# A graph layer's edge loop: groups taken in pairs, and one product that takes the transfer waits

## Chip, core and metric

One core of a Trainium2 chip runs the kernel. The core has a matrix engine (TensorE, called PE), a vector engine (DVE), a scalar engine (ACT), a general engine that also issues the indirect transfers (POOL), and a sync engine that issues the plain transfers (SP). Each has its own stream of instructions; they wait for one another by semaphores. Sixteen DMA engines move data between the chip's memory (DRAM) and the on-chip memory (SBUF); PE writes to PSUM, which has eight banks. The metric is the device time of one execution in microseconds (us).

## What is computed

A message-passing layer over a graph with 12500 nodes of 64 numbers and 200000 edges. `dst` is sorted.

```python
nodes = node_state[edges].reshape(num_edges, -1)          # x[src] | x[dst], 128 wide
gates = ssp(edge_state @ We1 + be1) @ We2 + be2
gates = gates * (1.0 - sigmoid(5.0 * (distance - 3.5)))
h = ssp(nodes @ Wn1 + bn1) @ Wn2 + bn2
messages = h * gates
message_sum = zeros_like(node_state).at[edges[:, 1]].add(messages)
new_state = node_state + (ssp(message_sum @ Ws1 + bs1) @ Ws2 + bs2)
out = layernorm(x + new_state)
```

`ssp(v)` is softplus less log 2. All arrays are fp32.

## The kernel before

**Groups.** The edges go through in 391 groups of 512 (`GE`), each in two halves of 256 (`HE`) and four columns of 128 (`K`). Because `dst` is sorted, the edges of one half touch a window of at most 42 neighbouring nodes (`W`). So `x[dst]` needs no gather: the lower half of Wn1 is multiplied with all nodes once, ahead of the loop (L508), and put in a table in DRAM; a half loads the 42 rows of its window, and a one-hot matrix picks the rows by a matrix product. The same one-hot matrix adds the messages up by node.

**One group, step by step.**

- `gather` (L186): four indirect transfers issued by POOL fetch `x[src]` of 128 edges each into `xg`. In twelve groups (`by_rows`) only three are indirect; the last 128 rows come one by one from SP (`fetch`, L201), four in each step of the loop.
- `load` (L207, L214): SP fetches the edge block `eT` and the two window rows `wns`.
- `onehot` (L219): DVE writes the one-hot columns beside the gathered ones.
- `transposes` (L227): PE transposes the four columns into the PSUM tile `tx`; `xcopy` (L232): ACT copies it to `xT`.
- `layer1_edge` (L236, L238) and `layer1_node` (L244): PE makes the first layers of gate and node net, 256 and 512 columns, into the PSUM tile `z` (two banks).
- `exps`, `logs` (L255, L258): ACT makes log(1 + exp(z)) over 768 columns; `softplus` (L263): DVE takes care of large values and writes `s`.
- `layer2_edge` (L269, L272), `layer2_node` (L278): PE makes the second layers into the PSUM tile `gh`.
- `hcut` (L287), `message` (L291): DVE multiplies by the cutoff and by each other.
- `scatter` (L295): PE multiplies messages and one-hot columns, into a free part of a `z` tile; `window` (L311): DVE adds the result to the running sums at the window's place, which it reads into a register with `window_bases` (L302).

That makes 28 products on PE for a group.

**Order.** The order is written out by hand. Step i of the loop handles several groups at different stages: second layer of group i-1, first layer of i+1, transposes of i+3, scatter of i-3, one-hot of i+5, load of i+5 and gather of i+16 (`AHEAD`). Each engine gets its instructions in the order in which the step writes them. The gather of group i+16 takes the buffer of group i-4 (20 buffers, `AHEAD + BEHIND`), so POOL waits there for the scatter of that group. The PSUM tiles z, gh and tx have two buffers each, eight banks in all. When all edges of a block of 512 nodes are done, the node net of that block is worked into the following steps in parts (`node_block`; L330 and L361 are its products). The last ten groups go in another order (`CATCH_UP`).

**Start.** Ahead of the loop stand the preparations: constants, the bases of the windows, the table, and the gathers of the first 16 groups.

Of the kernel before, what the change touches and what calls it, by code (L numbers as in the profile page):

```python
# [40 lines left out]
F32 = mybir.dt.float32  # L43
BF16 = mybir.dt.bfloat16
I32 = mybir.dt.int32
AF = mybir.ActivationFunctionType
OP = mybir.AluOpType
AX = mybir.AxisListType
PSUM = bass.MemoryType.PSUM
DRAM = bass.MemoryType.DRAM  # L50
DVE = mybir.EngineType.DVE
SP = mybir.EngineType.SP
# [4 lines left out]
P = 128  # L57
D = 64
HE = 256
GE = 2 * HE  # L60
W = 42
DW = D + W
PIECES = 3
NB = 512
K = 4
AHEAD = 16
LOADS = 5
SPREADS = 5
CATCH_UP = 10
PREPARE = 5  # L70
FREE = 7
BEHIND = 4

# [33 lines left out]
def gnn_resnorm_kernel(ctx: ExitStack, tc: tile.TileContext, a: dict, out: bass.AP, E: int):  # L107
# [16 lines left out]
    psum = ctx.enter_context(tc.tile_pool(name="psum", bufs=2, space=PSUM))  # L124

    def z_tile():
        return psum.tile([P, 2, NB], F32, name="z")

# [3 lines left out]
    def tx_tile():  # L132
        return psum.tile([P, NB], F32, name="tx")
# [31 lines left out]
    rs3 = const.tile([PIECES, K, D], BF16, name="rs3")  # L165
    wns = const.tile([DW, REST, 2, 2 * D], F32, name="wns")

# [5 lines left out]
    def padding(g, k):  # L173
        return g * GE + k % 2 * HE + k // 2 * P >= E

    def gather(g, after=False):

        xg = loads.tile([P, K, P], F32, name="xg", bufs=AHEAD + BEHIND)
        xgs[g] = xg
        if after:  # L180
            nc.vector.memset(xg[:, 0, :1], 0.0)
        for k in range(K - (g in by_rows)):
            if padding(g, k):
                nc.vector.memset(xg[:, k, :D], 0.0)
                continue
            nc.gpsimd.indirect_dma_start(  # L186
                out=xg[:, k, :D], out_offset=None, in_=x,
                in_offset=bass.IndirectOffsetOnAxis(ap=src_i[:, g, k : k + 1], axis=0))
# [13 lines left out]

    bases = {}

    def load(g):
        eTs[g] = loads.tile([P, HE], F32, name="eT")
        nc.sync.dma_start(eTs[g], a["eT"][:, g, :])  # L207
        if g % 2 == 0:
            _, at = nc.values_load_multi_w_load_instructions(
                base_i[0:1, 2 * g : 2 * g + 4], engines=[SP], min_val=0, max_val=N - 1,  # L210
                skip_runtime_bounds_check_because="they were clamped to these bounds")
            bases[g], bases[g + 1] = at[:2], at[2:]
        for h in range(2):
            nc.sync.dma_start(wns[D:DW, g % REST, h, :], table[bass.ds(bases[g][h], W), :])  # L214

    xTs, zs, us, ss, ghs, hs, msgs, scs = ({} for _ in range(8))

    def onehot(g):
# [3 lines left out]

    def transposes(g):
        tx = tx_tile()[:DW].rearrange("f (k e) -> f k e", k=K)
        for k in range(K):
            row = xrs[g][:, :DW] if g in by_rows and k == K - 1 else xgs[g][:, k, :DW]
            nc.tensor.transpose(tx[:, k, :], row, ident)  # L227
        xTs[g] = tx

    def xcopy(g):  # L230
        xT = work.tile([DW, K, P], F32, name="xT", bufs=3)
        nc.scalar.copy(xT, xTs[g])  # L232
        xTs[g] = xT.rearrange("f (t h) e -> f h t e", h=2)

    def layer1_edge(g):
        nc.tensor.matmul(zs[g][:, 0, :HE], be3.rearrange("q h d -> q (h d)"), ones3, start=True, stop=False,  # L236
                         skip_group_check=True)
        nc.tensor.matmul(zs[g][:, 0, :HE], we1.rearrange("a h d -> a (h d)"), eTs[g], start=False, stop=True,  # L238
                         skip_group_check=True)

    def layer1_node(g):
        for h in range(2):
            zn = zs[g][:, h, HE * (1 - h) : HE * (2 - h)]
            nc.tensor.matmul(zn, wns[:, g % REST, h, :], xTs[g][:, h], start=True, stop=True,  # L244
                             skip_group_check=True)
# [6 lines left out]
    def exps(g, part=every):  # L252
        if part.start == 0:
            us[g] = work.tile([P, 3 * HE], F32, name="u")
        nc.scalar.activation(us[g][:, part], z_of(g)[:, part], AF.Exp)  # L255
# [4 lines left out]
    def softplus(g, part=every):  # L260
        if part.start == 0:
            ss[g] = work.tile([P, 3, 2, P], F32, name="s", bufs=3)
        nc.vector.scalar_tensor_tensor(ss[g].rearrange("p i t e -> p (i t e)")[:, part], us[g][:, part], BIG,  # L263
                                       z_of(g)[:, part], OP.min, OP.max)

    def layer2_edge(g):
        gh = gh_tile()
        v = gh.rearrange("p (i t h d) -> p i t h d", i=2, t=2, h=2)
        nc.tensor.matmul(gh, ones3[:, :P], row3.rearrange("q i k d -> q (i k d)"), start=True, stop=False,  # L269
                         skip_group_check=True)  # L270
        for t in range(2):
            nc.tensor.matmul(v[:, 0, t], ss[g][:, 0, t, :], we2, start=False, stop=False, skip_group_check=True)  # L272
        ghs[g] = gh.rearrange("p (i k d) -> p i k d", i=2, k=K)

    def layer2_node(g):
        for h in range(2):
            for t in range(2):
                nc.tensor.matmul(ghs[g][:, 1, 2 * t + h, :], ss[g][:, 1 + h, t, :], wn2, start=False,  # L278
                                 stop=h == 1 and t == 1, skip_group_check=True)
# [5 lines left out]
    def hcut(g):  # L285
        hs[g] = work.tile([P, K, D], F32, name="h")
        nc.vector.tensor_mul(hs[g], ghs[g][:, 1], cut[:, g, :].to_broadcast([P, K, D]))  # L287

    def message(g):
        msgs[g] = work.tile([P, K, D], F32, name="msg", bufs=3)  # L290
        nc.vector.tensor_mul(msgs[g], ghs[g][:, 0], hs[g])  # L291

    def scatter(g, sc):
        for t in range(2):
            nc.tensor.matmul(sc, msgs[g][:, 2 * t : 2 * t + 2, :].rearrange("p h f -> p (h f)"),  # L295
                             xgs[g][:, 2 * t : 2 * t + 2, D:DW], start=t == 0, stop=t == 1, skip_group_check=True)
        scs[g] = sc

    window_at = {}

    def window_bases(g):
# [99 lines left out]
    with tc.manual_schedule():  # L401
# [3 lines left out]
        nc.sync.dma_start(src_i[:, AHEAD:, :], cols[:, AHEAD:, :])  # L405
        with tc.tile_pool(name="prep", bufs=1) as prep:
            dst_h = prep.tile([P, NR, HE], I32, name="dst_h")
# [19 lines left out]
            for g in range(AHEAD):  # L427
                if g < FREE:
                    gather(g)
                else:  # L430
# [10 lines left out]
            nc.scalar.dma_start(consts[:, FIRST:], a["consts"][:, FIRST:])  # L441
            nc.scalar.dma_start(wns[:D].rearrange("f r h o -> f (r h) o"),
                                a["Wn1"][:D, :].rearrange("f (r o) -> f r o", r=1).to_broadcast([D, 2 * REST, 2 * D]))

# [84 lines left out]

        with tc.tile_pool(name="finish", bufs=1) as finish:  # L530
            blocks = list(zip(node_blocks(N), block_steps(N, NG)))
# [9 lines left out]
            for i in range(-3, NG):  # L541
                second[i] = lagging(i, 1, (ends + 3,))
                third[i] = lagging(i, 3, (ends - 2, ends + 5))
                ahead[i] = [i + 3] if i < ends else [i + 2] if i == ends + 1 else [i + 1] if i > ends + 2 else []
            parts, begun, complete, rest = {}, None, 0, []

            def at(f, g, *more):
                if 0 <= g < NG:
                    f(g, *more)

            for g in range(LOADS - 3):
                load(g)
            for g in range(2):
                onehot(g)
            for i in range(-3, last - 1):
                now = parts.pop(i, [])
                early = [part for part in now if part.tensor]
                at(load, i + LOADS)
                fetch(i)
                if i >= 0:  # L560
                    at(gather, i + AHEAD, i < BEHIND)
                if i < ends:
# [49 lines left out]
                for part in now:  # L612
                    if not part.tensor:
                        part.others()
                complete = third[i][-1] + 1 if third[i] else 0
                if blocks and complete >= blocks[0][1] - PREPARE and not begun:
                    begun = node_block(*blocks[0][0], finish)
                    begun.pop(0).others()
                if blocks and complete >= blocks[0][1]:
                    steps = next(steps for steps in BLOCK_STEPS if i + steps[-1] < last - 1)  # L620
                    for n, part in zip(steps, begun):
                        parts.setdefault(i + n, []).append(part)
                    rest = begun[len(steps) :]
                    blocks.pop(0)
                    begun = None
            assert len(blocks) == 1 and begun and not parts
# [37 lines left out]
            for part in begun:  # L664
# [4 lines left out]
                         skip_runtime_bounds_check_because="a comparison's result")  # L669
    with tc.If(far > 0), tc.tile_pool(name="outside", bufs=1) as o:  # L670
        iota_n = o.tile([P, NB], F32, name="iota_n")
# [141 lines left out]
```

## Time and profile before

| what | before |
|---|---|
| median of three runs | 2455.14 us (2455.06 to 2465.51) |
| the profiled execution | 2482.05 us, its span 2480.3 us |
| mean granted clock of PE | 0.861 |
| PE busy | 2138.7 us, 86% of the span |
| POOL busy | 1473.3 us, 59%, 1555 instructions |
| DVE, ACT busy | 1087.5 us (44%), 920.1 us (37%) |
| DMA | 143.07 MB, mean 58 GB/s |
| first exp of the edge loop | 99 us after the start |
| last gather on POOL's timeline | starts at 2382 us |

The span runs from the first to the last instruction of the profiled execution; the time around it includes what lies before and after. "Busy" counts an engine while an instruction runs on it; a PE product's end is modelled, so a busy PE need not be at its full rate. The granted clock is the share of PE's full clock that the chip allowed. In the group rows, the number after the second bar is the idle time of the engine just ahead of these instructions, with what ended it: `<-PE z L244` means that the wait ended by a signal of PE about that product, `issue` means that the engine waited for nothing that the profile shows.

### The profile page before, as it was taken

How to read it: one execution, taken by the hardware profiler on the slowest of the kernel's cores; microseconds unless marked ns; L12 is line 12 of the kernel's file. 1: busy time of each engine (PE TensorE's matmuls, PEld its weight loads, DVE VectorE, ACT ScalarE, POOL GpSimd, SP SyncE). 2: the span in 40 equal slices, each digit the busy share in tenths (PEclk: the TensorE clock that was granted, in tenths of full speed). 3: DMA queues.
4: the chain of work that ended last, by engine and by line, in shares of the span. 5: the costliest groups of instructions: out<-in, count | busy, mean ns of one | idle time of the engine just before them, and what ended most of it. 6: DMA issues, size and time to landing. Idle time of an engine off the chain costs nothing.

```text
span 2480.3 us, 41084 instructions
## 1 busy us (share of the span) xinstructions
PE 2138.7 (86%) x11373; PEld 1741.1 (70%) x11373; DVE 1087.5 (44%) x2744; ACT 920.1 (37%) x1317; POOL 1473.3 (59%) x1555
## 2 busy tenths in 40 slices
PE   3888898889888989888988988888889888888897
PEld 3767677777767777767767776677767676676775
DVE  3334434444344344444444444444444444444455
ACT  1223333333333333433433333433333333433443
POOL 6656666666666666666666666666665656666620
PEclk9988879887888878898897888988887989988898
DMA  6322222222222222222222222222222222222220
GB/s 187 111 50 53 51 51 52 53 52 51 53 51 55 53 51 53 55 53 53 55 54 56 52 53 55 55 56 55 53 57 55 50 55 56 57 60 55 55 53 22
DMA packets 170982, 143.07 MB, mean 58 GB/s; under 512 B 46475, under 2 KB 142915, under 8 KB 170746
## 3 DMA queue, kind: packets, MB, share of 16 engines
q1 hardware_dynamic: 119746, 87.95, 12.3%
q0 software_dynamic: 49632, 50.92, 11.5%
q10 hardware_dynamic: 1368, 1.51, 0.3%
q8 instruction: 93, 1.52, 0.3%
q14 instruction: 143, 1.17, 0.2%
HBM read 130.57 MB, written 9.63 MB: 57 GB/s over the span
## 4 chain that ended last, share of the span: by engine, by line
PE 79%; issue 9%; DVE 5%; ACT 3%; another core or an unknown queue 3%; DVEq 1%; DMA 1%; SPq 0%; ACTq 0%
PE z L244 17%; PE gh L278 12%; PE gh L272 11%; PE z L238 11%; PE tx L227 8%; PE z L295 8%; PE gh L269 4%; PE z L236 3%; PE tx L330 2%; DVE h L287 1%; DVE msg L291 1%; ACT u L255 1%; DVE sums L311 1%; PE z L508 1%
## 5 line engine op out<-in xcount | busy, mean ns | idle before, releaser
L186 POOL DMA_INDIRECT xg<-in_x,src_i x1551 | 1473.1, 950 | 909.8 <-issue 360.3
L255 ACT ACTIVATE u<-z 128x768 f32<-128x768 f32 x392 | 317.4, 810 | 1435.4 <-PE z L244 466.8
L287 DVE TENSOR_TENSOR h<-gh,cut 128x256 f32<-128x256 f32 x391 | 166.0, 425 | 1154.0 <-PE z L244 357.8
L244 PE MATMUL z<-xT,wns 106*128 106x256 f32 x1564 | 498.4, 448 | 3.8 <-issue 1.6
L278 PE MATMUL gh<-consts,s 128*128 128x64 f32 x3128 | 429.6, 285 | 7.4 <-issue 7.4
L278 PEld LDWEIGHTS gh<-consts,s 128*128 128x128 f32 x3128 | 424.1, 210 | 6.9 <-issue 6.8
L272 PE MATMUL gh<-consts,s 128*128 128x128 f32 x1564 | 308.9, 325 | 133.8 <-issue 124.4
L244 PEld LDWEIGHTS z<-xT,wns 106*128 106x128 f32 x1564 | 353.0, 227 | 72.7 <-issue 4.2
L272 PEld LDWEIGHTS gh<-consts,s 128*128 128x128 f32 x1564 | 227.6, 210 | 240.4 <-issue 224.8
L263 DVE SCALAR_TENSOR_TENSOR s<-u,z 128x768 f32<-128x768 f32 x392 | 372.7, 951 | 24.3 <-ACT u L258 12.3
L258 ACT ACTIVATE u<-u,one 128x768 f32<-128x768 f32 x392 | 365.9, 934 | 12.7
L227 PE MATMUL tx<-consts,xg 128*106 128x128 f32 x1552 | 279.9, 308 | 61.0 <-ACT u L258 25.6
L238 PE MATMUL z<-eT,consts 128*128 128x256 f32 x782 | 313.9, 487 | 0.0
L295 PEld LDWEIGHTS z<-xg,msg 128*128 128x128 f32 x1512 | 279.8, 230 | 41.1 <-issue 8.2
L295 PE MATMUL z<-xg,msg 128*128 128x84 f32 x1512 | 263.4, 301 | 14.5 <-issue 14.2
L227 PEld LDWEIGHTS tx<-consts,xg 128*106 128x106 f32 x1552 | 211.3, 160 | 86.8 <-issue 46.0
L232 ACT COPY xT<-tx 106x512 f32<-106x512 f32 x391 | 221.6, 567 | 18.4 <-PE tx L227 11.2
L311 DVE TENSOR_TENSOR sums<-sums,z 64x42 f32 x756 | 148.7, 197 | 129.9 <-issue 118.4
L291 DVE TENSOR_TENSOR msg<-gh,h 128x256 f32<-128x256 f32 x391 | 165.8, 424 | 13.4
L238 PEld LDWEIGHTS z<-eT,consts 128*128 128x128 f32 x782 | 131.4, 211 | 54.1 <-issue 15.4
L269 PE MATMUL gh<-row,ones 3*128 3x512 bf16 x391 | 157.1, 402 | 2.7 <-DVE msg L291 2.6
L219 DVE TENSOR_TENSOR xg<-consts,rel 128x168 f32<-128x168 f32 x391 | 137.0, 351 | 0.1
(100 smaller groups left out, 621.4 us busy)
## 6 DMA issues: line engine op xcount, KB each, us to landing
eT<-in_eT SPq DMA_DIRECT2D x391, 128.0 KB
xg<-in_x,src_i POOLq DMA_INDIRECT x1551
xr<-in_x SPq DMA_DIRECT2D x1536, 0.2 KB
wns<-table SPq DMA_DIRECT2D x782, 21.0 KB
table<-tb SPq DMA_DIRECT2D x14, 448.0 KB
sums<-in_xT SPq DMA_DIRECT2D x7, 455.0 KB
y<-in_x SPq DMA_DIRECT2D x24, 128.0 KB
out<-y SPq DMA_DIRECT2D x24, 128.0 KB
```

The source lines that it names most:

```text
L186: nc.gpsimd.indirect_dma_start(out=xg[:, k, :D], out_offset=None, in_=x, in_offset=bass.IndirectOffsetOnAxis(ap=src_i[:, g, k : k + 1], ax ...
L227: nc.tensor.transpose(tx[:, k, :], row, ident)
L232: nc.scalar.copy(xT, xTs[g])
L238: nc.tensor.matmul(zs[g][:, 0, :HE], we1.rearrange("a h d -> a (h d)"), eTs[g], start=False, stop=True, skip_group_check=True)
L244: nc.tensor.matmul(zn, wns[:, g % REST, h, :], xTs[g][:, h], start=True, stop=True, skip_group_check=True)
L255: nc.scalar.activation(us[g][:, part], z_of(g)[:, part], AF.Exp)
L258: nc.scalar.activation(us[g][:, part], us[g][:, part], AF.Ln, bias=one)
L263: nc.vector.scalar_tensor_tensor(ss[g].rearrange("p i t e -> p (i t e)")[:, part], us[g][:, part], BIG, z_of(g)[:, part], OP.min, OP.max)
L269: nc.tensor.matmul(gh, ones3[:, :P], row3.rearrange("q i k d -> q (i k d)"), start=True, stop=False, skip_group_check=True)
L272: nc.tensor.matmul(v[:, 0, t], ss[g][:, 0, t, :], we2, start=False, stop=False, skip_group_check=True)
L278: nc.tensor.matmul(ghs[g][:, 1, 2 * t + h, :], ss[g][:, 1 + h, t, :], wn2, start=False, stop=h == 1 and t == 1, skip_group_check=True)
L295: nc.tensor.matmul(sc, msgs[g][:, 2 * t : 2 * t + 2, :].rearrange("p h f -> p (h f)"), xgs[g][:, 2 * t : 2 * t + 2, D:DW], start=t == 0, s ...
```

## The change

The loop takes two groups, 2k and 2k+1, in one turn k. There are 184 such turns (groups 0 to 367); the last 23 groups go through the old loop (`SINGLE`).

- The gathers of a pair, eight of them, are issued together at the start of turn k, for pair k+7 (`AHEAD` 14, `BEHIND` 6). A pair has one buffer, and there are ten of them.
- The window rows and the edge blocks of a pair lie in one tile, `wins`, with four slots; SP issues four transfers for the window rows and one for both edge blocks, for pair k+2.
- A new small product, `probe`, stands first on PE in each turn. It reads one column of each of the eight gathers of pair k+1 and of the five transfers of pair k, so that it waits for all of them; its result is used by nothing.
- PE's order in a turn is: probe, the eight transposes of pair k+1, the second node half of layer 1 of both groups of pair k, then edge net and first node half of each, both second layers of pair k-1, a node block's product where there is one, and the two scatters of pair k-2.
- The z tile with two buffers becomes three banks z0, z1, z2 with one buffer each, and a fourth bank, sc, takes the scatters. Bank z1 holds the second node halves of both groups.
- ACT and DVE answer in `respond`: copies of the transposes, then exp, log and softplus of pair k-1 bank by bank (512 wide instead of 768), then `hcut` and `message` of pair k-2 and `window` of pair k-3. Of two groups the later one is read first.
- The window's place is read into registers once for a pair (`pair_bases`).
- A few buffers more: xT 4, h 3, msg 4.

```diff
-AHEAD = 16
-LOADS = 5
+AHEAD = 14
+LOADS = 6
+SINGLE = 21
-BEHIND = 4
+BEHIND = 6
...
     def gather(g, after=False):
-        xg = loads.tile([P, K, P], F32, name="xg", bufs=AHEAD + BEHIND)
-        xgs[g] = xg
+        if g // 2 not in pair_x:
+            pair_x[g // 2] = loads.tile([P, 2, K, P], F32, name="xg", bufs=(AHEAD + BEHIND) // 2)
+        xg = xgs[g] = pair_x[g // 2][:, g % 2]
...
+    def load(k):
+        gs = [g for g in (2 * k, 2 * k + 1) if g < NG]
...
+        edges = wins[:, k % (REST // 2), 4 * P :].rearrange("p (g e) -> p g e", g=2)
...
         for h in range(2):
-            nc.sync.dma_start(wns[D:DW, g % REST, h, :], table[bass.ds(bases[g][h], W), :])
+            for g in reversed(gs):
+                nc.sync.dma_start(wns(g)[D:DW, h, :], table[bass.ds(at[g % 2 * 2 + h], W), :])
+        nc.sync.dma_start(edges[:, : len(gs)], a["eT"][:, 2 * k : 2 * k + len(gs), :])
...
+    def probe(k, tx):
+        n = K - any(g in by_rows for g in (2 * k + 2, 2 * k + 3))
+        columns = pair_x[k + 1][:DW, :, :n, D - 1]
+        fetched = wins[:DW, k % (REST // 2), : 5 * P].rearrange("p (n c) -> p n c", c=P)[:, :, 0]
+        nc.tensor.matmul(tx[:5, : 2 * n].rearrange("f (g k) -> f g k", g=2), fetched, columns, start=True, stop=True,
+                         skip_group_check=True)
...
+            def activate(k, bank, pool):
+                z, s = pair[k][bank]
+                u = pool.tile([P, NB], F32, name="ub", bufs=3)
+                nc.scalar.activation(u, z, AF.Exp)
+                nc.scalar.activation(u, u, AF.Ln, bias=one)
+                return lambda: nc.vector.scalar_tensor_tensor(s, u, BIG, z, OP.min, OP.max)
+
+            def respond(k, now):
+                if k >= 0:
+                    xcopy(2 * k + 1)
+                    xcopy(2 * k)
+                if k >= 1:
+                    for bank in (1, 0, 2):
+                        activate(k - 1, bank, finish)()
+                backwards(hcut, k - 2)
+                backwards(message, k - 2)
+                backwards(window, k - 3)
+                for f in now:
+                    f()
...
+            turns = (last - SINGLE) // 2
+            late = []
+            with tc.tile_pool(name="z_pairs", bufs=1, space=PSUM) as pairs:
+                for k in range(-1, turns):
+                    steps = (2 * k, 2 * k + 1)
+                    load(k + 2)
+                    for i in steps:
+                        fetch(i)
+                    if k >= 0:
+                        backwards(gather, k + AHEAD // 2, k < BEHIND // 2)
...
+                    respond(k, now)
+                    both(onehot, k + 2)
+                    if k >= 2:
+                        pair_bases(2 * k - 4)
+
+                    both(transposes, k + 1, k if k >= 0 else None)
+                    if k >= 0:
+                        z = [pairs.tile([P, NB], F32, name=f"z{bank}") for bank in range(3)]
+                        soft = [finish.tile([P, NB], F32, name="sb", bufs=6) for _ in range(3)]
...
+                        both(layer1_node, k, (1,))
+                        for g in (2 * k, 2 * k + 1):
+                            layer1_edge(g)
+                            layer1_node(g, (0,))
+                    both(layer2, k - 1)
+                    if product or k >= 2:
+                        sc = pairs.tile([P, NB], F32, name="sc")
+                    if product:
+                        product(sc[:, 4 * W :])
+                    if k >= 2:
+                        for n in range(2):
+                            scatter(2 * k - 4 + n, sc[:, 2 * W * n : 2 * W * (n + 1)])
+                    blocks_begin(2 * k + 1, 2 * k - 4)
+                respond(turns, late)
+            phase.enter_context(z_tiles("z_single"))
+            for i in range(2 * turns - 1, last - 1):
...
+                at(gather, i + AHEAD + 1)
```

`both` and `backwards` call a step for the two groups of a pair, the earlier or the later first.

## Prediction

> **What bounds the kernel now.** I read the page first. Its first part says TensorE, its chain of waits says the same, and I do not believe either.
>
> ```profile
> PE 2138.7 (86%) x11373; PEld 1741.1 (70%) x11373; DVE 1087.5 (44%) x2744; ACT 920.1 (37%) x1317; POOL 1473.3 (59%) x1555
> ...
> PE 79%; issue 9%; DVE 5%; ACT 3%; another core or an unknown queue 3%; DVEq 1%; DMA 1%; SPq 0%; ACTq 0%
> ```
>
> A PE row runs until the next matmul may end, so 86% need not be 86% of work. The windows view tests that: the main loop against a stretch after the last gather (it starts at 2382 us).
>
> ```profile
> 300.00:2300.00 2000.00, 1758.35 (x9375) 1431.13 (x9374) 881.36 (x2219) 759.69 (x1084) 1238.02 (x1306) 0.85 0.23 54
> 2400.00:2430.00 30.00, 28.51 (x183) 22.41 (x182) 17.87 (x49) 14.40 (x21) 0.00 (x0) 1.00 0.20 56
> ```
>
> The columns are busy time with count for PE, weight loads, DVE, ACT and POOL, then the granted clock, DMA share and GB/s. A group has 28 matmuls. In the tail, 183 in 30 us are 4.6 us for 28, and the exps there are 4.35 to 4.5 us apart; in the loop, 9375 in 2000 us are 6.0 us for 28. So PE can do a group in about 4.4 us and takes 6.0 wherever gathers run.
>
> Next, is it the clock? Two group periods, 12 us apart, at half and at full clock:
>
> ```profile
> 1213.00:1219.07 6.07, 6.06 (x25) 4.86 (x23) 2.48 (x6) 2.22 (x3) 3.83 (x5) 0.50 0.23 53
> ...
> 1225.14:1231.21 6.07, 5.88 (x36) 4.86 (x36) 2.47 (x6) 2.22 (x3) 3.78 (x4) 1.00 0.29 72
> ```
>
> At 0.50 PE falls behind and catches up at 1.00 (25 records, then 36), while ACT and DVE keep one group per 6.07 us. The clock is not the pacemaker. POOL's timeline (start, length, idle before and what ended it) shows what is:
>
> ```profile
> 228.79 0.94 POOL L186 DMA_INDIRECT xg<-in_x,src_i  x1 [1.35 <-PE z L244]
> ...
> 233.49 0.94 POOL L186 DMA_INDIRECT xg<-in_x,src_i  x1 [1.25 <-PE z L244]
> ...
> 1202.18 0.94 POOL L186 DMA_INDIRECT xg<-in_x,src_i  x1 [1.22 <-PE z L244]
> 1203.43 0.95 POOL L186 DMA_INDIRECT xg<-in_x,src_i  x1 [0.30 <-issue]
> ...
> 1208.27 0.94 POOL L186 DMA_INDIRECT xg<-in_x,src_i  x1 [1.39 <-PE tx L227]
> ...
> 1477.45 0.95 POOL L186 DMA_INDIRECT xg<-in_x,src_i  x1 [2.71 <-PE z L295]
> ...
> 1489.21 0.94 POOL L186 DMA_INDIRECT xg<-in_x,src_i  x1 [2.08 <-PE z L238]
> ```
>
> These are starts of bursts. A burst of 3 gathers (a by-rows group) lasts 4.70 us to the next, one of 4 lasts 6.09, and one of 8, where POOL had two groups' buffers at once, 11.76. Inside a burst a gather costs 0.95 + 0.30 = 1.25 us, and then POOL stands 1.2 to 2.7 us until a PE signal arrives. That signal is late, not the product:
>
> ```profile
> L186 POOL DMA_INDIRECT xg<-in_x,src_i x1551 | 1473.1, 950 | 909.8 <-issue 360.3
> L255 ACT ACTIVATE u<-z 128x768 f32<-128x768 f32 x392 | 317.4, 810 | 1435.4 <-PE z L244 466.8
> L287 DVE TENSOR_TENSOR h<-gh,cut 128x256 f32<-128x256 f32 x391 | 166.0, 425 | 1154.0 <-PE z L244 357.8
> ```
>
> L255's exps follow the product they need by 5.3 us (median) and L287's by 2.8, and POOL, ACT and DVE start again together: in the same timeline ACT's L255 starts at 1208.03, L287 at 1208.26, the gather at 1208.27. So the loop is a cycle: burst of gathers, a drain in which PE's signals come through, next burst. Period = c + m x gathers. From 4 and 3: m = 6.07 - 4.70 = 1.37 to 1.4; from the prologue's one burst of 12 (116.38 to 134.06, 17.68 us) against 4: (17.68 - 6.09)/8 = 1.449. With m = 1.44, c = 0.3 us.
>
> **The change, part by part.** The profiled run took 2482.05 us (span 2480.3); the median of the runs shown is 2455.14, so results are scaled by 0.989.
>
> **Pairs.** Eight gathers go out in one burst per turn, and only the first waits. c is paid once for two groups: 0.3 + 8 x 1.44 = 11.82 us instead of 2 x 6.07 = 12.14. The before trace holds four natural bursts of 8: 11.75, 12.16, 12.09, 11.76, mean 11.94. I take 11.85, between the fit and that mean and nearer the fit, as the bursts of 8 there had single-group work under them. 184 turns x -0.29 = **-53 us**. Bounds: below, POOL's own 8 x 1.25 = 10.0 us; above, see the slower rival.
>
> **One product takes the DMA waits.** A group has 7 PE products that wait for a transfer (four L227, one L238, two L244). PE's waits on transfers in the loop add up to 3.5 us in the whole run, three waits; so what is spared on PE's path is nearly nothing. The probe adds one small product per turn, nearest row L278 at 285 ns, and six or seven wait-only instructions, nearest row an ACT semaphore instruction of 17 ns: 0.3 to 0.4 us. PE has two groups at 4.4 = 8.8 + 0.4 = 9.2 us of work in an 11.85 us turn, so this is covered; uncovered it is 184 x 0.4 = 70 us. All of the turn's PE work stands behind the probe. What it waits for is old: the gathers were issued six turns (71 us) before, the loads two turns (24 us) before.
>
> **Fewer signals.** PE raises 10 semaphore increments per group now, 6 per pair after. If the price of 1.44 against POOL's 1.25 per gather is PE's signals pushing in among gathers, m falls too: at most to 1.25 (-394 us in the loop), at least to nothing. The trace has no row for it; the bursts of 8 and 12, with fewer signals let through, still give 1.44, so I take nothing.
>
> **Order of reading, ACT and DVE.** The second of two products is read first, so one wait serves both. ACT has per pair 2 copies at 0.567 and three exp and log passes 512 wide; scaled from 768 wide (810 and 934, by the copy's 567 for 512 about 0.58 and 0.72) 1.13 + 3.9 = 5.0 us against 4.63 now; DVE has three softplus passes of about 0.68 for two of 0.951, +0.14. Both lie inside 11.85 at 42 to 50%. The register load per group (L311 waits 118.4 us for issue in 756) becomes one per pair: off the path, nothing.
>
> **SP.** Per pair four window rows and one edge block instead of four and two, plus the same eight row fetches. SP issues them beside POOL; nothing on the path (SP's own largest wait is 41.3 us for L201).
>
> **z banks single.** layer1 of pair k now waits until softplus of pair k-1 has read the same bank. The chain: copies 1.13, first bank's exp and log 1.30, softplus 0.68, together 3.1 us after the drain; PE fills 2.5 us of that with eight transposes at 0.308. A stall of about 0.6 us; 9.2 + 0.6 = 9.8 is still under 11.85, which is why I cost it at nothing. It is the margin that the slower rival eats.
>
> **Ahead 14 for 16, and the ends.** Eight more gathers come after the prologue: 8 x 1.44 = +11.5; the tail without gathers is one group shorter, -4.4: **+7**. Passing from pairs to the last 23 single groups drains the banks once: one response chain, **+5** (estimate from the 3.1 us above). Sum: -53 + 7 + 5 = -41; 2441 profiled, x 0.989 = **2414 us**.
>
> [...]
>
> ```profile
> 126.42 0.22 PE L278 MATMUL gh<-consts,s 128*128 128x64 f32 x1 [0.77 <-issue]
> 127.84 0.22 PE L278 MATMUL gh<-consts,s 128*128 128x64 f32 x1 [1.21 <-issue]
> 129.26 0.22 PE L278 MATMUL gh<-consts,s 128*128 128x64 f32 x1 [1.19 <-issue]
> ```
>
> 10 us into a burst PE gets one product per 1.42 us. [...]
> [...]
>
> **Rivals.** With e the +12 of the ends:
> - **Signals set the price, and they are fewer**: m between 1.25 and 1.44. At 11.45 us per turn: 184 x -0.69 + 12 = -115, 2341 after scaling; at POOL's floor of 10.0, 2077. For it: idle of 0.30 at "issue" is all that POOL shows inside bursts. Against: bursts of 8. Chance 0.14.
> - **The gap goes with gathers, not bursts**: 12.0 to 12.14 per turn, 2442 to 2467 (no change that can be told). For it: two of four natural bursts at 12.1. Chance 0.13.
> - **Slower: the pair's turn does not fit a burst**. PE's products issued late in the burst crawl; the last signals (z2, gh, sc) come after the drain, and with single banks the chain of 3.1 us is then bare, followed by the rest of PE's turn. 9.2 + 3.1 = 12.3, and at a half clock in the refill (25 records for 28 per 6.07 us) up to 1 us more; 12.6 gives 184 x 0.46 + 12 = +97, 2551. It decides from 12.07 us per turn (12 us / 184 below 12.14), only 0.2 above my value. For it: single banks and the rows at 126 us. Chance 0.37.
> - My forecast, 11.7 to 12.0: 0.36.
>
> **How the numbers follow.** This kernel's runs spread by 0.4%, so 0.5% is what can be told from no change. Faster is the forecast and the first rival, 0.50; same 0.13; slower 0.37. The likeliest case alone spans 2386 to 2440; with the bound of m at 11.4 and a stalled turn of 12.65 the range is 2330 to 2560, leaving out POOL's floor and turns over 12.65.
>
> **What would show it.** POOL's burst starts 11.7 to 12.0 us apart with one idle of about 2 us after the eighth gather: right. Idle over 3 us there, ending at PE sc or z, with ACT waiting for the same: the slower rival. Bursts 10.0 to 11.5 apart: the price was in the signals. PE waiting at the probe for a transfer: my covering of that wait is wrong. A tail of more than 100 us after the last gather: the +7 and +5 are.

## Result and profile after

The changed kernel takes 2672.89 us (median of 4 runs, 2668.49 to 2683.59) against 2460.32 us of the kernel before: ratio 1.0859, 95% interval 1.0795 to 1.0923. A second comparison on a chip that behaves alike gave 1.0874 (1.081 to 1.0938), and its trace is used below beside the first. The forecast of 2414 us was wrong in sign, and the time lies above its range.

The profiled run took 2668.49 us, 186 more than the one of before. From the page of the changed kernel, the busy row and the row of the gathers:

```profile
PE 2323.5 (87%) x11741; PEld 1775.4 (67%) x11741; DVE 1061.4 (40%) x2928; ACT 1007.3 (38%) x1685; POOL 1469.6 (55%) x1555
...
L206 POOL DMA_INDIRECT xg<-in_x,src_i x1551 | 1469.4, 947 | 1093.6 <-PE sc L351 531.6
```

POOL does the same work as before but idles 1094 instead of 910 us, now waiting for the scatter. Its timeline shows first gathers of bursts (start, length, idle before):

```profile
1202.72 0.94 POOL L206 DMA_INDIRECT xg<-in_x,src_i  x1 [2.11 <-PE sc L351]
...
1214.62 0.95 POOL L206 DMA_INDIRECT xg<-in_x,src_i  x1 [2.08 <-remote]
...
1226.55 0.94 POOL L206 DMA_INDIRECT xg<-in_x,src_i  x1 [2.26 <-PE sc L351]
...
596.75 0.94 POOL L206 DMA_INDIRECT xg<-in_x,src_i  x1 [2.22 <-PE sc L351]
...
615.70 0.94 POOL L206 DMA_INDIRECT xg<-in_x,src_i  x1 [9.28 <-PE sc L351]
```

The first two turns last 11.90 and 11.93 us, what was forecast. The turn from 596.75 lasts 18.95. Over the whole loop, 133 of the 174 bursts of eight come to the next within 13 us (mean 12.04, median 11.96), and 41 do not (mean 17.18). The mean burst of four before was 6.135 us, 12.27 a pair. So the ordinary turns give 133 x -0.23 = -31 us, the long ones 41 x 4.91 = +201, and twelve turns with seven gathers (11.58 against 10.81 us) +9; about +7 remain for the two ends. The loss is in one turn of four.

What happens there is seen in the windows of three turns in a row (busy us with count for PE, weight loads, DVE, ACT, POOL, then the granted clock):

```profile
584.70:596.60 11.90, 9.18 (x56) 7.01 (x56) 4.76 (x14) 4.81 (x8) 7.54 (x8) 1.00 0.17 34
596.60:615.50 18.90, 16.82 (x61) 12.67 (x61) 6.01 (x18) 4.91 (x8) 7.54 (x8) 0.51 0.20 49
615.50:627.50 12.00, 10.25 (x61) 8.03 (x59) 3.55 (x10) 4.82 (x8) 7.55 (x8) 0.93 0.21 49
```

In the middle one PE does the products of a turn at half clock: 16.8 us of them instead of 9.2. The timeline of SP and PE shows how this turn began:

```profile
596.16 0.01 SPq L235 DMA_DIRECT2D wins<-table  x1
596.17 0.03 SPq L236 DMA_DIRECT2D wins<-in_eT  x1
...
598.68 0.20 PE L245 MATMUL tx<-xg,wins 106*5 106x8 f32 x2 [2.95 <-DMA wins<-in_eT]
```

SP issued the load of this pair at 596.17, when PE already stood at the probe; it should have been two turns earlier. From 596.80 on the clock was at half. Three readings fit these lines: SP is too slow and PE only fills the wait (called theory SP below); the half clock is the loss and SP's lateness is incidental (theory clock); or the single wait for all transfers is what holds PE up (theory probe).

Not every long turn begins so. For the next one the edge block was issued at 966.73, 13.6 us before the probe, and PE went from the probe into the transposes without a wait:

```profile
966.73 0.00 SPq L236 DMA_DIRECT2D wins<-in_eT  x1
...
980.36 0.21 PE L245 MATMUL tx<-xg,wins 106*5 106x8 f32 x2
...
998.76 0.94 POOL L206 DMA_INDIRECT xg<-in_x,src_i  x1 [8.38 <-PE sc L351]
```

The windows of the turn before it and of this turn:

```profile
968.30:980.40 12.10, 9.63 (x60) 7.48 (x60) 6.26 (x18) 5.62 (x10) 7.65 (x8) 0.95 0.15 29
980.40:998.40 18.00, 18.00 (x64) 13.55 (x63) 5.93 (x17) 5.03 (x8) 7.54 (x8) 0.50 0.21 50
```

PE is busy for all of the 18.00 us at clock 0.50, about twice the 9.18 us of the turn from 584.70 at full clock, and POOL stands until the scatter at its end. So PE at half clock is enough for a long turn. A count over both traces says how often it is which:

| the 41 long turns | first trace | second trace |
|---|---|---|
| PE waits for one of SP's transfers at the probe or the transposes | 16 turns, 88 us over 12.27 | 5 turns, 34 us |
| edge block issued 8 us or more before the probe, no such wait | 15 turns, 61 us | 26 turns, 116 us |
| neither | 10 turns, 52 us | 10 turns, 52 us |
| 13 us or more of the turn at half clock | 34 turns | 35 turns |

No ordinary turn has more than 7.4 us at half clock. PE's turns with the edge block issued 10 us or more ahead (87 in the first trace, 111 in the second) took 12.44 and 12.78 us on average, the others 13.85 and 13.80, without the first eight: late loads go with longer turns, but turns without them are still longer than the 12.27 of before. In the kernel before the clock was also at half, for 693 us in all, but in five stretches only for 17 us or longer; here it is 976 us, with 36 such stretches. The clock fell after idle of PE: in the 3.4 us before the 73 falls between 310 and 2300 us PE idled 2.0 us on average (0.9 to 3.4), against 0.37 in 3.4 us of that stretch at large; 3.41 us is the shortest time for which the clock kept one value in this trace and in that of before.

What SP gets done can be counted too. SP's instructions, of all kinds, that start within each 1.25 us of a burst are 5.7, 5.5, 3.7, 3.1, 1.9, 2.9, 2.7, 2.1 from the first gather to the eighth: SP gets less through late in a burst than early. An ordinary turn lets 26.1 through in its burst and 9.0 in the drain, **35.1**. The program needs **41.4**: 15 for the window rows and the edge block (register operations, moves, transfers, one register load and a wait), two row fetches of 13, and 0.4 on average for the node blocks. A long turn lets 63.0 through. In the kernel before, a burst of four with its drain let 18.5 + 5.2 = 23.7 through, 47.4 per pair, all that it had to issue. So SP falls behind in ordinary turns and catches up in long ones. That a share of (41.4 - 35.1)/(63.0 - 35.1) = 0.23 of the turns must then be long (it was 41 of 174, 0.24) says no more: the program's instructions have to be issued, whatever makes the turns long. SP's waits, the largest for its window loads and the largest for PE:

```profile
SPq L235 <- DMA wins<-table: 56.3, 68, 1.4
...
SPq L235 <- PE tx L264: 2.8, 8, 0.4
```

The first is put down to its own earlier transfers. Waits for PE, for a slot to come free, are 6.8 us in the run: SP was hardly ever far enough ahead to be stopped. Between 310 and 2300 us SP had no pause longer than 1.4 us, yet its pauses of 0.5 to 1.4 us add up to 607 us; what it stood for in most of them the trace does not say.

### The profile page after: what moved, and what is told of

The parts are those of the page before. It is cut to its first block, busy times and chain, and to the rows that moved or that the text cites. A ratio compares the mean times of both kernels' runs of the same rounds, so it can differ in the third digit from the quotient of the medians.

```text
span 2666.6 us, 42513 instructions
## 1 busy us (share of the span) xinstructions
PE 2323.5 (87%) x11741; PEld 1775.4 (67%) x11741; DVE 1061.4 (40%) x2928; ACT 1007.3 (38%) x1685; POOL 1469.6 (55%) x1555
## 3 DMA queue, kind: packets, MB, share of 16 engines
q1 hardware_dynamic: 91674, 87.94, 11.6%
## 5 line engine op out<-in xcount | busy, mean ns | idle before, releaser
L646 DVE SCALAR_TENSOR_TENSOR sb<-ub,z 128x512 f32<-128x512 f32 x552 | 379.0, 687 | 962.2 <-ACT ub L645 454.8
L300 PE MATMUL z<-xT,wins 106*128 106x256 f32 x1564 | 562.8, 474 | 0.0
L644 ACT ACTIVATE ub<-z 128x512 f32<-128x512 f32 x552 | 329.1, 596 | 457.2 <-remote 214.2
L334 PE MATMUL gh<-consts,sb 128*128 128x64 f32 x2944 | 425.4, 295 | 0.0
L334 PEld LDWEIGHTS gh<-consts,sb 128*128 128x128 f32 x2944 | 418.2, 219 | 0.0
L300 PEld LDWEIGHTS z<-xT,wins 106*128 106x128 f32 x1564 | 369.6, 249 | 58.8 <-ACT xT L272 0.9
L645 ACT ACTIVATE ub<-ub,one 128x512 f32<-128x512 f32 x552 | 398.3, 722 | 17.9
L351 PE MATMUL sc<-xg,msg 128*128 128x84 f32 x1456 | 253.0, 304 | 113.4 <-issue 89.5
L295 PE MATMUL z<-wins,consts 128*128 128x256 f32 x782 | 325.2, 503 | 0.0
L328 PE MATMUL gh<-consts,sb 128*128 128x128 f32 x1472 | 298.1, 331 | 0.0
L328 PEld LDWEIGHTS gh<-consts,sb 128*128 128x128 f32 x1472 | 220.6, 215 | 98.2 <-issue 98.2
```

Source lines behind the costliest of these rows:

```text
L295: nc.tensor.matmul(z_edge(g), we1.rearrange("a h d -> a (h d)"), eTs[g], start=False, stop=True, skip_group_check=True)
L300: nc.tensor.matmul(z_node(g, h), wns(g)[:, h, :], xTs[g][:, h], start=True, stop=True, skip_group_check=True)
L328: nc.tensor.matmul(v[:, 0, t], s_edge(g, t), we2, start=False, stop=False, skip_group_check=True)
L334: nc.tensor.matmul(ghs[g][:, 1, 2 * t + h, :], s_node(g, h, t), wn2, start=False, stop=h == 1 and t == 1, skip_group_check=True)
L644: nc.scalar.activation(u, z, AF.Exp)
L645: nc.scalar.activation(u, u, AF.Ln, bias=one)
```

## Experiments

Seven of the eight comparisons made here ran on chips where the kernel before takes 1993 to 2004 us, and POOL issues a gather every 1.25 us without any drain. They are called chips without the hold-up; the first measurements, one later comparison and the profiles above are of chips with it. All ratios are to the kernel before on the same chip.

**First set (no hold-up).** Rows fetched singly: `ROWS = 4` becomes `ROWS = 1`; fewer groups have their last column fetched so.

> The changed kernel with the rows that SP fetches singly cut from eight to two per pair (three groups instead of twelve have their last column fetched so; nine more indirect gathers). Theory SP: with bursts of eight, SP gets some 35 instructions through in a fast turn of 11.8 us and needs 43, so the loads come late, the probe waits, PE idles and the clock halves. With some 25 instead of 43 instructions the loads should lead the probe by over 15 us always, turns over 13 us should nearly go (56 of 180 now), and the time be about 2673 - 212 + 13 = 2475 us. Theory clock: PE's regular idle of 2 to 3 us at the end of each turn halves the clock whatever SP does; the time stays at 2680 or above. Theory probe (one wait for all transfers is what holds PE up): as theory SP where lateness goes, about 2475.

2014.64 us, ratio 1.0084 (1.006 to 1.0108). Products in PE's idle time, which add work that is used by nothing:

```diff
+FILL = 8
...
+                        for n in range(FILL):
+                            nc.tensor.matmul(sc[:, 4 * W + HE :], ident, consts[:, : NB - 4 * W - HE], start=True,
+                                             stop=True, skip_group_check=True)
```

> The changed kernel with eight extra products of 88 columns, used by nothing, at the end of PE's turn (about 2 us, in the idle before the next turn). Theory clock: the clock stays at full, turns of 16 us go, and the time is about 2673 - 212 = 2460 to 2480 us. Theory SP: the turns stay as slow as SP's instructions, whether PE idles or not: 2600 to 2700 us, with PE waiting at the probe for a load.

2255.11 us, 1.1292 (1.1259 to 1.1324). A turn is 10.86 us here: without the hold-up the changed kernel leaves PE little idle (in its run on such a chip, below, PE is busy 1546.59 of the 1600 us from 300 on), so PE became the bound. One turn of slack: `AHEAD = 12`, `BEHIND = 8`.

> The changed kernel with AHEAD 12 and BEHIND 8 instead of 14 and 6: the gathers of a turn wait for a scatter one turn earlier. Theory clock (a slow PE turn holds POOL up because the scatter stands last in the turn): slow turns are taken up by the slack, 11.5 to 12 us a turn on average, 2400 to 2470 us. Theory SP: POOL runs ahead, SP gets still less through, 2670 us or more.

2015.4 us, 1.0085 (1.0061 to 1.0109). No probe: `both(transposes, k + 1)`.

> The changed kernel without the probe: each product waits for its own transfer. Theory probe: the transposes and the node halves no longer wait for the last load, 2 to 5% faster than the changed kernel. Theories SP and clock: what comes late is needed 3 us later in the turn anyway; within 1.5% of the changed kernel, 2640 to 2710 us.

2003.99 us, 1.0023 (1.0009 to 1.0037). None of these tells the theories apart, since the loss itself is absent.

**Both kernels again (a chip with the hold-up), and two that were to change the bursts.**

> The changed kernel once more, beside the kernel before on the same chip: the first four experiments ran on a chip where the kernel before took 2001 us instead of 2460 and POOL issued gathers every 1.25 us without a pause. Theory SP with clock: what the pairs lose, they lose only where gathers hold up the other engines' instructions and signals; on such a chip the ratio is about 1.09 again, on a chip like that of the first experiments POOL's issue sets the time, 8 x 1.25 = 10.0 us per pair in both kernels, and the ratio is 1.00 to 1.01. Theory probe (the pairs' order itself or the wait for all transfers costs PE time): the ratio is 1.03 or more on either chip.

2678.3 us, ratio 1.0874 (1.081 to 1.0938).

> The kernel before with a profile, on the same chip. On a chip where POOL's gathers follow each other at 1.25 us without a drain the bursts of four vanish and the loop takes 5.0 us per group (about 2000 us); where a drain of 1.4 us follows each burst of four it takes 6.07 (about 2460 us).

2463.94 us; bursts of four 5.98 us apart (median).

> The kernel before with the gathers of two groups issued together in every second step (AHEAD 15, BEHIND 5), and nothing else changed. Theory SP: where gathers hold up the others, bursts of eight starve SP here too; with 47 instructions per pair it is slower than the kernel before by 3% or more. Theory clock: SP does not matter and PE's order is that of before; 0.3 + 8 x 1.44 = 11.85 us per pair, 1 to 3% faster than before. Where POOL issues without a pause: within 0.5%.

```diff
-                if i >= 0:
-                    at(gather, i + AHEAD, i < BEHIND)
+                if i >= 0 and i % 2 == 0:
+                    for n in range(2):
+                        at(gather, i + AHEAD + n, i < BEHIND)
```

2472.35 us, ratio 1.0024 (0.9993 to 1.0055). A miss: 327 bursts were still of four, because each group's first gather still waits for a PE signal of its own, and that came only after a drain. It does not test bursts of eight in every turn; of the 15 single ones after 130 us, 14 last 11.7 to 12.1 us and one 17.99.

> The changed kernel with each turn's gathers in two bursts of four, the second released in mid-turn by a small DVE write after the second bank's softplus. Theory SP: two drains per turn let SP's instructions through as before; where gathers hold up the others, about 12.2 to 12.6 us per turn, 2480 to 2560 us. Theory clock: PE's idle stays at the end of the turn and so do the turns at half clock, 2600 us or more. Where POOL issues without a pause: POOL waits in mid-turn, 2010 to 2150 us.

```diff
-                        backwards(gather, k + AHEAD // 2, k < BEHIND // 2)
+                        gather(2 * k + AHEAD + 1, k < BEHIND // 2)
...
                     for bank in (1, 0, 2):
                         activate(k - 1, bank, finish)()
+                        if bank == 0 and k < turns:
+                            gather(2 * k + AHEAD, True)
...
+                    if k == 0:
+                        gather(AHEAD, True)
```

2712.96 us, 1.101 (1.0947 to 1.1074). A miss too: DVE's release came before the first four gathers were out, 173 bursts stayed at eight, and 35 us were lost for a reason that stays open.

**The first set once more**, meant for a chip with the hold-up; it ran on one without.

> Two instead of eight rows per pair fetched singly by SP, as before; now wanted on a chip where gathers hold the others up (kernel before about 2460, changed kernel 2675). Theory SP: the loads lead the probe by over 15 us always, turns over 13 us nearly go, about 2475 us. Theory clock: SP does not matter, 2680 us or above. On a chip where POOL issues without a pause: 1.008 of before again.

2015.81 us, 1.0067.

> Eight products of 88 columns, used by nothing, at the end of PE's turn; on the chip of the first experiments they made a turn of 10.9 us with POOL waiting, so they cost PE 2 us and fit in 11.94. Theory clock: the clock stays full, slow turns go, 2460 to 2480 us. Theory SP: 2600 to 2700 us, PE waiting at the probe for a load. On a chip where POOL issues without a pause: 1.129 of before again.

2251.36 us, 1.1247.

> The gathers wait for a scatter one turn earlier (AHEAD 12, BEHIND 8). Theory clock: the slack takes up the turns at half clock, 2400 to 2470 us. Theory SP: POOL runs ahead and SP gets less through, 2670 us or more. On a chip where POOL issues without a pause: 1.008 of before again.

2014.95 us, 1.0077.

> Without the probe. Theory probe: 2 to 5% faster than the changed kernel, 2545 to 2625 us. Theories SP and clock: within 1.5% of it, 2640 to 2710 us. On a chip where POOL issues without a pause: 1.002 of before again.

2003.85 us, 1.0029. The fewer rows were tried on two more chips, none with the hold-up:

> Two instead of eight rows per pair fetched singly by SP; still wanted where gathers hold the others up (kernel before about 2465, changed kernel 2678). Theory SP: the loads lead the probe by over 15 us, turns over 13 us nearly go, about 2475 us. Theory clock: 2680 us or above. Where POOL issues without a pause: 1.007 of before again.

2019.57 us, 1.0075.

> Two instead of eight rows per pair fetched singly by SP, wanted where gathers hold the others up (before about 2465, changed kernel 2678). SP then needs some 24 instructions per pair; a turn with a burst of eight let 35 through in the changed kernel's traces there. Theory SP: the loads lead by over 15 us, turns over 13 us nearly go, 2460 to 2500 us. Theory clock: 2660 us or above. Where POOL issues without a pause: 1.007 of before again.

2013.85 us, 1.0103. Half the rows (`ROWS = 2`) also met a chip without it:

> The changed kernel with four instead of eight rows per pair fetched singly by SP (six groups instead of twelve; six more gathers): 30 instead of 42 instructions of SP per pair. Where gathers hold the others up: theory SP: a turn with a burst of eight lets 35 through, so the shortage is gone with this half step already, 2460 to 2500 us; theory clock: 2660 us or above. Where POOL issues without a pause: between the changed kernel and the one with two rows, ratio 1.004 to 1.010, 6 x 1.25 us above the changed kernel.

2017.62 us, 1.0085 (1.0053 to 1.0117). So what fewer rows do where the loss is has not been measured.

**Does the change itself cost anything?**

> The changed kernel where POOL issues without a pause (kernel before about 2000 us): the probe and the pairs' order cost nothing there if theory SP or clock is right, and the time is that of its variants there, 2000 to 2020 us, ratio 1.00 to 1.01. If the ratio is 1.03 or more, the probe costs PE time by itself, since the kernel without it took 2004. Where gathers hold the others up (before about 2465): 2678 again.

2001.78 us, ratio 1.0046 (1.0023 to 1.0068). The 8.6% are there only with the hold-up. SP's timeline shows the difference in how long it takes over its transfers (start, length from the first to the last); first the changed kernel with the hold-up:

```profile
1203.20 7.99 SPq L221 DMA_DIRECT2D xr<-in_x  x8
...
1214.08 3.24 SPq L235 DMA_DIRECT2D wins<-table  x4
```

Without it, and then its largest wait for PE there:

```profile
990.11 3.80 SPq L221 DMA_DIRECT2D xr<-in_x  x8
1003.79 1.87 SPq L235 DMA_DIRECT2D wins<-table  x4
```

```profile
SPq L235 <- PE z L300: 326.3, 181, 9.0
```

The eight row fetches take 3.80 us here and 7.99 there, and here SP then waits for a free slot in 181 turns, 326 us in all, against 6.8 us with the hold-up.

**The dose.** If SP is the cause, giving it more to do should bring the same picture on a chip without the hold-up (`ROWS = 8`, twelve gathers fewer):

> The changed kernel with sixteen instead of eight rows per pair fetched singly by SP (24 groups instead of 12 have their last column fetched so; twelve fewer indirect gathers). Where gathers hold the others up (before about 2465): theory SP: some 79 instead of 43 instructions per pair at the 3.3 per us that SP got through there make 20 us or more per turn, above 3000 us; theory clock: SP does not matter, 2678 - 12 x 1.44 = 2660 us. Where POOL issues without a pause: SP's turn grows from about 5.5 us by 8 x 0.41 to 8.8 of 10.0 us, twelve gathers of 1.25 us less: 1987 us, ratio about 0.996.

2406.33 us, ratio 1.2042 (1.1999 to 1.2086). The part of this expectation for such a chip was wrong: SP has 65 instructions per pair (not 79), and they take longer than I added up. The timeline of SP in this run:

```profile
1003.88 2.04 SPq L235 DMA_DIRECT2D wins<-table  x4
1005.96 0.37 SPq L236 DMA_DIRECT2D wins<-in_eT  x1
1007.29 7.68 SPq L221 DMA_DIRECT2D xr<-in_x  x16
1015.83 1.87 SPq L235 DMA_DIRECT2D wins<-table  x4
...
1019.08 7.31 SPq L221 DMA_DIRECT2D xr<-in_x  x16
1027.24 1.87 SPq L235 DMA_DIRECT2D wins<-table  x4
```

A pair takes SP 11.95 and 11.41 us, and the mean of the last 180 turns is 11.78; between 310 and 1850 us SP has no pause above 0.4 us. Yet no turn need be like the mean: 146 turns take 10.06 us and 34 take 19.16, of which 17.45 at half clock. So SP alone can make quick turns and long ones at half clock. It is not the slow kernel's case in every point: here the edge block was issued 8 us or more before the probe in only 4 of the 34 long turns, and with the hold-up in at least 15 and 26 of the 41. The last question on such chips is whether it is the half clock that costs. The same with the eight products in PE's idle:

> Sixteen rows per pair for SP and eight products at the end of PE's turn that nothing uses. Where POOL issues without a pause, sixteen rows alone took 2406 us with a clock of 0.85 and the eight products alone 2251 to 2255. Theory SP: SP's own pace (11.4 to 11.8 us for a pair's instructions) sets the time and the half clock only fills the wait; with the clock kept up by the products it is still 2370 to 2440 us. Theory clock: the half clock is the loss; 2240 to 2300 us, that of the products alone. Where gathers hold the others up both expect more than 2678, by SP's instructions or by PE's load.

2409.72 us, 1.208 (1.2049 to 1.2111). The view of cores (span and mean granted clock) of sixteen rows alone, then with the products:

```profile
core 0: 2402.9 us, clock 0.848
```

```profile
core 0: 2407.1 us, clock 0.946
```

The mean clock rose from 0.848 to 0.946 and the time at half clock fell from 733 to 263 us, and the kernel took the same 2406 to 2410 us; of the turns over 13 us, 12 were left of 34, and the others rose from 10.06 to 11.09 us. With SP's pauses at 0.4 us and below in the run of sixteen rows, the better clock bought nothing. With the hold-up, where SP does pause and the loads are mostly in time, this was not run.

## Why the prediction was wrong, step by step

- **What bounds the kernel**: right, as far as it went. The cycle of burst and drain was read from POOL's rows, and ordinary turns of 12.04 us (median 11.96) stand against the forecast of 11.85.
- **The step that failed: PE's 9.2 us in an 11.85 us turn, "so this is covered", with the half clock given nothing.** The 9.2 us hold at full clock only. In 14 turns of the first trace and 16 of the second, PE is busy throughout and at half clock throughout, and they take 16.7 us each, or 18.1 with the products of a node block. This is more than 11.85, it ends with the scatter for which POOL's next burst waits (9.28 and 8.38 us in the rows above), and no turn with eight gathers is shorter than 11.83, so that nothing makes it up. The long turns, 34 of 41 with 13 us or more at half clock, are +201 us, more than the whole loss of 186. The rows of before had the figure: 25 of 28 records in 6.07 us at half clock are 6.8 us a group and 13.6 a pair, over 11.85 already. The prediction took from them that PE catches up. That was so before, where stretches of 17 us or more at half clock were five; in the pairs there were 36.
- **"The clock is not the pacemaker"** was read from two windows 12 us apart. In the pairs the clock fell after PE's idle (2.0 us in the 3.4 us before). In ordinary turns PE idles 1.6 us on average, at the probe and between the products of the scatter. Which idle brings the long stretches, and why 43 of the 94 stretches at half clock in the first trace last 3.4 us and 36 last 17 and more, some with PE busy throughout, stays open.
- **"SP issues them beside POOL; nothing on the path"** is wrong as well, though the traces lay less of the loss on it. SP's small waits were taken as a sign of room. The pairs need 41.4 instructions of SP, and the natural bursts of eight in the trace of before let 41.0 through (32.2 and 8.8) in 11.94 us: no room at all. In the pairs it was 35.1. PE's waits for SP's transfers lie in 16 and in 5 of the 41 long turns. If SP's rate in each kind of turn were fixed, the 6.3 instructions that an ordinary turn leaves over would hold the mean near 12.04 + 6.3 x (17.23 - 12.04)/(63.0 - 35.1) = 13.2 us even at a full clock (an estimate from the counts; 17.23 is the long turns' mean in the stretch that was counted). So a better clock alone might have gained little. No run separates the two.
- **Pairs pay the drain once**: right in size for the ordinary turns, 0.23 us a pair below before against a forecast of 0.29. The drain and the first two gathers of a burst are when SP gets most of its instructions through (9.0, 5.7 and 5.5 of the 35.1), and with one burst instead of two there is less of both.
- **"What it waits for is old"**: wrong for the loads. They were to lead the probe by 24 us; the lead was 11.6 us on average and 1.4 at the least. The probe then waited for the edge block 38.1 us in 16 turns. The probe's own cost was rightly put at nothing: without the hold-up the ratios are 1.0023 and 1.0029 without it and 1.0046 with it, on different chips and with intervals that overlap. With the hold-up that was not run.
- **Fewer signals**: nothing was forecast, and the ordinary turns show nothing.
- **Single z banks, ACT, DVE**: covered, in the ordinary turns with the hold-up and, without it, in turns of eight gathers at 1.25 us (PE busy 1546.59 of 1600 us).
- **The ends**: +12 forecast, some +7 left over in the sum above. The tail after the last gather is 104 us against 98.
- **Products that come slowly late in a burst**: the slower rival took them from the rows at 126 us, 1.42 us apart. Of the four bursts of eight in the trace of before, which held 44, 45, 51 and 59 products of PE, one reached the 57 that a pair needs; that a turn's products fit a burst was the author's estimate. The same spacing did come, at the end of a turn:

```profile
594.09 0.23 PE L351 MATMUL sc<-xg,msg 128*128 128x84 f32 x1 [0.68 <-DMA xg<-in_x,src_i]
595.50 0.23 PE L351 MATMUL sc<-xg,msg 128*128 128x84 f32 x1 [1.17 <-issue]
```

  Products of the scatter are 1.41 us apart. The rows do not tell what is behind it. The ordinary turn of 11.90 us from 584.70 contains it, and the 1.17 us are part of PE's idle before the clock falls at 596.80.
- **The slower rival** had the sign, a price of 12.6 per turn, and a half clock that costs up to 1 us. Measured were 13.25 us per burst of eight, made of ordinary turns and of long ones that cost 4.9 us each. Its other causes, late signals and bare single banks, cannot be more in an ordinary turn than the 0.19 us by which it exceeds 11.85.

Open: fewer rows, slack or filled idle were not tried on a chip with the hold-up. There it is shown by the traces that the loss lies in turns at half clock; what brings them about, PE's idle alone or SP's lateness as well, is argued. That SP alone can make such turns is shown only without the hold-up. No version ran faster than the kernel before.

## What to carry over

Work that is "covered" at full clock need not be covered at half (here 9.2 us a turn by the forecast, 16.7 as measured at half). Where the trace shows a half clock at all, take PE's sum at that clock too, and ask whether the change leaves longer stretches of it. Count the instructions of every issuing engine per turn and hold them against what the trace lets through, not only busy shares and waits. But a count that has to come out, because all the work is done in the end, is no proof of a cause: look at the long turns one by one, and see whether what the theory calls late was late there.

## What was not expected of the hardware

- The kernel before took 2460 and 2467 us in the comparisons with the hold-up and 1993 to 2004 in the others (medians). With the hold-up, SP's instructions come some 0.7 us apart late in a burst (in the turn from 1202.72: 1209.77, 1210.49, 1211.18, 1211.91, 1212.62 us), and POOL stands after each burst, by the median 1.36 us in the kernel before and 2.31 us in the changed one (310 to 2300 us); without it neither is seen (the eight row fetches take SP 3.80 us, above), and the 1471 last gathers of the changed kernel follow each other in one unbroken burst. What makes the chips differ no run here shows.
- SP got 41 instructions through in a natural burst of eight before the change and 35 in one after it. Why the pairs let fewer through is open.
- PE stayed at half clock for 17 us and more at a time, 36 times in the first trace, also while its rows show it busy throughout (18.00 us from 980.40). Why is open.
